# Background steps of an attention loop sorted by the engine they need, and a layernorm's small operations on GpSimd

## The chip, the cores and the metric

The kernel runs on one core of one Trainium2 chip. The metric is the device time of one launch in microseconds (us), the median of several runs. The core's engines are TensorE (PE; its weight loads are listed as PEld), VectorE (DVE), ScalarE (ACT), GpSimd (POOL) and SyncE (SP), which issues the DMAs. Each engine works through its own queue in order.

## The reference, cut to what matters

```python
x = x + 0.5 * ffn(layernorm(x))          # x: 4 batches of 1024 tokens, 128 wide
x = x + attn(layernorm(x))
x = x + 0.5 * ffn(layernorm(x))
# attn: its own layernorm h of its input (with scale and bias); c_q, c_kv = h @ w_down.T (64 latents each);
#       16 heads of 64 from the latents, rope on q and k, softmax(q k / 8) v, w_out, plus its input
# ffn:  8 experts; router weights from sigmoid(x @ Wr / temperature), zone test, a top-2 fallback;
#       sum over experts of weight * (silu(x Wg) * (x Wu)) Wd
# layernorm: (x - mean) / sqrt(var + 1e-5)
```

All is float32. The attention scores of 64 (batch, head) pairs over 1024 x 1024 tokens are the bulk of the work.

## The kernel before, in words

The program runs in three stages: the first feed-forward layer (until about 250 us), the attention loop (until about 1610 us) and the second feed-forward layer. The order on every engine is written out by hand: nothing is rescheduled.

**The attention loop** (in `run`) has groups g = 0 to 128 of four score slots each. A slot is one pair of heads, 512 queries and 128 keys. A unit is 8 slots, so two groups; a batch is 128 slots, so 32 groups. In each group, for n = 0 to 15, TensorE makes one matmul for each of two heads of the scores (`score`, L700: high and low parts of Q and K, then the maximum's row); at the fourth of a slot ScalarE takes the exponential (L704) and, with both heads done, GpSimd adds it to a sum (`accumulate`, L716). Between them, at n = 0, 7, 13 and behind n = 15, `passA` makes scores for the row maxima of a later unit in the two banks `psA` (L675) and VectorE reduces them (L676); the next such matmul must wait for that reduction, as there is one pair of banks. Then come the rope's matmuls (L595, even groups) or the output projection (`outp`, L756, odd groups), the fourth maximum, a background step, in even groups the denominator (`den`, L735, which reads GpSimd's sum), then VectorE's part of the rope (L583, four products) or of the output (L764, eight adds), and last the values of the four slots before (`values`, L723, into bank `psC`). The banks of the scores go round over `psS[0..3]` and `psX`; rope and output use `psX` and `psS[3]`; `den` uses `psS[0]`, and the steps' own matmuls get `self.rest = [self.psS[1]]` through `aux`.

GpSimd also has two rope sums (L600, L602) and a remainder (L611) in every second group. SP issues, in its order, the Q/K loads of later head pairs (16 in two groups), the latents for the rope, its stores, the maximum's way through DRAM (L679 to maxr) and the denominator's (L741, L743, read as dT by L760).

**Background steps** are generators that yield between steps. `attn_pre(b)` for batches 1 to 3 makes the two layernorms and the latents of a batch: statistics (`stats`: `bn_stats` L209, `bn_aggr` L212, the addition of EPS L213, all VectorE), `power` (L216, GpSimd, variance to the power -1/2), `norm` (L222 on VectorE forms -mean times that power, then ScalarE L227 applies it), transposes (L540), latents (L546, VectorE L552 and L553 split them into a high and a low part), a transpose of the key latents (L561) and the stores to `c_scr`. Each half of a batch has its own stages, 9 steps apart. `ffn_pre` does the same for the second feed-forward layer (transposes L256, router logits L269), then `route` (L293 to L348: ScalarE, GpSimd and a dozen small VectorE operations) and `weight_rows` (L357). It starts for batches 0, 1 and 2 in groups 42, 74 and 106.

`step(boundary)` picks a step in turn from the two streams (1: `ffn_pre`, 2: `attn_pre`). A generator yields True ahead of a step that needs TensorE; such a step runs only at `step(True)`, at the group's end. `step(False)` stands at n = 7 and n = 13. So there are three steps a group at most. For batches 2 and 3, `attn_pre` waits at stage 24 until the batch before last is done, and yields True until then.

In the first stage `bg1` and in the last `bg2` call the same generators by fixed rates.

Of the kernel before, what the change touches and what calls it, by code (L numbers as in the profile page):

```python
# [30 lines left out]
PBUFS = 8  # L31
NROPE = 9
# [5 lines left out]
class Kernel:  # L38
# [165 lines left out]


    def stats(self, st, src, mv, rstd, half):
# [3 lines left out]
        if half:  # L210
            for i in range(4):
                nc.vector.bn_aggr(mv[:, i, :], st[:, i, :])  # L212
            nc.vector.tensor_scalar(rstd[:, :, 1], mv[:, :, 1], EPS, None, ALU.add)  # L213

    def power(self, rstd):
        self.nc.gpsimd.tensor_tensor(rstd[:, :, 0], rstd[:, :, 1], self.neghalf[:, :4], ALU.pow)  # L216

    def norm(self, out, src, mv, rstd, half, vector=False):

        nc = self.nc  # L220
        if not (half or vector):
            nc.vector.scalar_tensor_tensor(rstd[:, :, 1], mv[:, :, 0], -1.0, rstd[:, :, 0], ALU.mult, ALU.mult)  # L222
# [7 lines left out]
    def ffn_pre(self, P, blks, xs, w_out, done=None, rows=None):  # L230
# [8 lines left out]
        def stage(k, h, blk):  # L239
# [5 lines left out]
            if k in (0, 1):  # L245
                self.stats(st["st", h], src, mv[:, hs], rstd[:, hs], k)
            elif k == 3:
                self.power(rstd[:, hs])
# [23 lines left out]
        for k in range(14 + 5 * (n - 1)):  # L272
            yield any(k - 5 * h in (8, 12) for h in range(n))
# [7 lines left out]
    def route(self, P, T, z, w_out):  # L281
# [9 lines left out]
        more = (None,) if self.slot >= 0 else ()  # L291
        yield
# [3 lines left out]
        yield  # L296
# [11 lines left out]
        yield  # L308
        v.reciprocal(dx, dx)
        yield  # L310
# [5 lines left out]
        yield  # L316
# [6 lines left out]
        yield  # L323
        g = new("g", [E, E], "f0")
        v.tensor_tensor(g, fb.unsqueeze(2).to_broadcast(sh4), below, ALU.is_gt)
        yield
        v.tensor_reduce(le, g, AX.X, ALU.add)
        yield
# [6 lines left out]
        yield  # L335
# [6 lines left out]
        yield  # L342
        v.tensor_tensor(w, w, fb, ALU.add)
        v.tensor_reduce(s, w, AX.X, ALU.add)
        yield
# [4 lines left out]
    def weight_rows(self, P, b):  # L350
# [4 lines left out]
        yield True  # L355
# [4 lines left out]
        yield  # L360
# [141 lines left out]
    def attn_pre(self, b):  # L502
# [9 lines left out]
        def stage(k, h):  # L512
# [6 lines left out]
            if k in (0, 1):  # L519
                assert 2 * b + h in self.done  # L520
                self.stats(st["st", h], src, mv[:, q], rstd[:, q], k)
            elif k == 2:
                self.power(rstd[:, q])
# [4 lines left out]
            elif k in (7, 8):  # L528
                self.stats(st["st", h], [y[:, i, :] for i in range(4)], mv2[:, q], rstd2[:, q], k - 7)
            elif k == 9:  # L530
                self.power(rstd2[:, q])
# [32 lines left out]
        for k in range(25 + 9):  # L564
            yield any(k - 9 * h in (14, 17, 20, 24) for h in range(2))
            while k == 24 and b >= 2 and self.slot < 128 * (b - 1) + 4:
                yield True
# [159 lines left out]
    def den(self, U):  # L727
# [3 lines left out]
        pd = self.psS[0]  # L731
# [36 lines left out]
    def run(self):  # L768
# [93 lines left out]
        self.rest, self.rope_banks, self.bankO = [self.psS[1]], [self.psX, self.psS[3]], [self.psX, self.psS[3]]  # L862
# [4 lines left out]
        def step(boundary):  # L867

            for _ in range(2):
                k = 1 + turns["next"] % 2  # L870
                turns["next"] += 1
                while streams[k] and streams[k][0] not in needs:
# [3 lines left out]
                    else:  # L876
                        needs[streams[k][0]] = v
                if streams[k] and (boundary or not needs[streams[k][0]]):
                    gen = streams[k][0]
# [139 lines left out]
```

## Time and profile before

| | us |
|---|---|
| median of 3 runs | 1769.61 (1763.7, 1769.61, 1775.22) |
| the profiled execution's own time | 1774.69 |
| its span, first to last instruction | 1772.9 |
| PE busy in the span | 1677.2 (95%) |
| DVE busy | 1304.0 (74%) |
| ACT busy | 925.2 (52%) |
| POOL busy | 1460.5 (82%) |
| row maxima on DVE, L676, 512 of 1224 ns | 626.7 |
| sums on POOL, L716, 320 of 2375 ns and 64 of 2390 ns | 912.9 |
| values on PE, L723, 2048 of 604 ns | 472.7 |

The profile is of one execution. Busy time is the sum of an engine's instructions; matmuls overlap, so a busy PE is not a PE at its peak. The waits view names, for each line, what ended the idle time before it. The windows view gives busy time in chosen stretches, with the granted clock of TensorE. Line numbers are those of the kernel before, unless the text says otherwise.

### The profile page before, as it was taken

The page shows a single profiled execution, that of the slowest core. Times are in us where ns is not written, and L with a number is a line of the kernel's source. Part 1 is how long each engine was busy: PE and PEld are TensorE (multiplying, and loading weights), DVE is VectorE, ACT ScalarE, POOL GpSimd, SP SyncE. Part 2 cuts the span into 40 slices and gives each one's busy share as a digit, 9 for nine tenths or more (in the row PEclk, how much of TensorE's full clock was granted, in tenths as well). Part 3 has the DMA queues.
Part 4 walks back from the last instruction along what each step waited for, and adds up shares of the span by engine and source line. Part 5 has one row for each costly group of instructions (what it writes and reads, how often), then busy time and mean ns, then how long its engine had stood idle before and what let it go on. Part 6 is the DMA issues. An engine that isn't in the chain of part 4 may idle for free.

```text
span 1772.9 us, 31230 instructions
## 1 busy us (share of the span) xinstructions
PE 1677.2 (95%) x11428; PEld 1043.0 (59%) x11428; DVE 1304.0 (74%) x2223; ACT 925.2 (52%) x1916; POOL 1460.5 (82%) x803
## 2 busy tenths in 40 slices
PE   7988978999999999999999999999999999899998
PEld 5777755555455555455555555655655555456777
DVE  6776658777777778777887777787777766744887
ACT  4666554556455455455444555544555544445555
POOL 4448778989889989889989899898999977576666
PEclk9999989999999999999999999999999999999999
DMA  6025446554544554445445545544545542024443
GB/s 200 1 72 175 134 131 155 144 144 120 143 121 121 135 153 120 120 132 144 117 115 139 146 126 147 131 125 112 130 121 148 127 98 61 2 86 109 141 124 103
DMA packets 241417, 216.00 MB, mean 122 GB/s; under 512 B 156784, under 2 KB 169712, under 8 KB 240624
## 3 DMA queue, kind: packets, MB, share of 16 engines
q1 hardware_dynamic: 241264, 214.01, 44.9%
q8 instruction: 90, 1.47, 0.4%
q14 instruction: 63, 0.52, 0.1%
HBM read 129.93 MB, written 84.02 MB: 121 GB/s over the span
## 4 chain that ended last, share of the span: by engine, by line
PE 72%; DVE 12%; POOL 5%; ACT 3%; issue 3%; DMA 2%; SPq 2%; POOLq 0%; DVEq 0%; ACTq 0%
PE psc L723 21%; PE ps_s L700 17%; PE ps_a L675 9%; PE psx L700 5%; DVE m L676 4%; PE ps_s L402 3%; PE ps_s L735 3%; PE ps_s L481 3%; POOL acc L716 2%; PE psx L436 2%; PE psx L756 2%; SPq L47 2%; PE psx L595 2%; DVE X L764 1%; PE psc L373 1%
## 5 line engine op out<-in xcount | busy, mean ns | idle before, releaser
L676 DVE TENSOR_REDUCE m<-ps_a 128x2 f32<-128x1024 f32 x512 | 626.7, 1224 | 327.5 <-PE ps_a L675 326.6
L716 POOL TENSOR_TENSOR acc<-acc,p 128x1024 f32<-128x1024 f32 x320 | 760.0, 2375 | 53.7 <-ACT p L704 34.5
L704 ACT ACTIVATE p<-ps_s 128x512 f32<-128x512 f32 x896 | 494.2, 599 | 370.2 <-PE ps_s L700 359.5
L700 PE MATMUL ps_s<-QT,KT 64*128 64x512 f32 x2688 | 478.1, 398 | 3.1 <-DVE X L764 2.1
L723 PE MATMUL psc<-p,ckn 128*64 128x512 f32 x2048 | 472.7, 604 | 0.0
L700 PEld LDWEIGHTS ps_s<-QT,KT 64*128 64x128 f32 x2688 | 314.5, 187 | 50.7 <-DVE X L764 3.4
L723 PEld LDWEIGHTS psc<-p,ckn 128*64 128x64 f32 x2048 | 136.8, 138 | 266.4 <-issue 265.5
L675 PE MATMUL ps_a<-KT,QT 64*128 64x512 f32 x1024 | 247.8, 476 | 37.5 <-DVE m L676 37.4
L716 POOL TENSOR_TENSOR acc<-p 128x1024 f32<-128x1024 f32 x64 | 152.9, 2390 | 98.0 <-ACT p L704 98.0
L675 PEld LDWEIGHTS ps_a<-KT,QT 64*128 64x128 f32 x1024 | 98.7, 185 | 208.6 <-DVE m L676 95.8
L700 PE MATMUL ps_s<-maxr,one_row 64*128 64x512 f32 x896 | 206.2, 394 | 0.0
L611 POOL TENSOR_TENSOR eo<-eo,hi_r 128x1024 fp32r<-128x1024 f32 x64 | 153.2, 2394 | 1.4 <-ACT hi_r L607 1.3
L725 ACT COPY osb<-psc 128x512 f32<-128x512 f32 x64 | 37.6, 587 | 189.0 <-PE psc L723 189.0
L386 POOL TENSOR_TENSOR X<-X,dtmp 128x512 f32<-128x512 f32 x54 | 69.2, 1282 | 66.1 <-ACT dtmp L385 59.6
L700 PE MATMUL psx<-QT,KT 64*128 64x512 f32 x384 | 111.9, 398 | 0.0
L700 PEld LDWEIGHTS ps_s<-maxr,one_row 64*128 64x128 f32 x896 | 99.7, 186 | 11.5
L489 POOL TENSOR_TENSOR p<-eo,p 128x512 fp32r<-128x512 f32 x42 | 63.0, 1505 | 43.8 <-ACT p L488 35.8
L600 POOL TENSOR_TENSOR eo<-rt,rt 128x512 f32<-128x512 f32 x64 | 82.8, 1294 | 5.5 <-DVE rt L583 5.4
L602 POOL TENSOR_TENSOR eo<-rt,rt 128x512 f32<-128x512 f32 x64 | 82.4, 1288 | 0.0
L764 DVE SCALAR_TENSOR_TENSOR X<-ps_s,rT,X 128x128 f32<-128x128 f32 x252 | 70.9, 344 | 13.5 <-PE ps_s L756 7.5
L700 PEld LDWEIGHTS psx<-QT,KT 64*128 64x128 f32 x384 | 72.1, 188 | 12.1
L704 ACT ACTIVATE p<-psx 128x512 f32<-128x512 f32 x128 | 77.6, 606 | 1.2 <-ACT p L704 0.6
(195 smaller groups left out, 2502.5 us busy)
## 6 DMA issues: line engine op xcount, KB each, us to landing
C_l<-cs SPq DMA_DIRECT2D x64, 512.0 KB
QT<-qs SPq DMA_DIRECT2D x256, 128.0 KB
KT<-ks SPq DMA_DIRECT2D x256, 128.0 KB
qs<-hi_r SPq DMA_DIRECT2D x32, 512.0 KB
qs<-eo SPq DMA_DIRECT2D x32, 512.0 KB
ks<-hi_r SPq DMA_DIRECT2D x32, 512.0 KB
ks<-eo SPq DMA_DIRECT2D x32, 512.0 KB
wb<-wt SPq DMA_DIRECT2D x64, 256.0 KB
```

The source lines that it names most:

```text
L386: nc.gpsimd.tensor_tensor(X[:, t:t + 4, :], X[:, t:t + 4, :], tmp, ALU.add)
L489: (nc.gpsimd if m < N - 1 else nc.vector).tensor_tensor(sh[:, 1, :], hp, self.f(sh[:, 0, :]), ALU.subtract)
L600: nc.gpsimd.tensor_tensor(w["eo"][:, 0, :], w[0, 0], w[1, 1], ALU.subtract)
L602: nc.gpsimd.tensor_tensor(w["eo"][:, 1, :], w[0, 1], w[1, 0], ALU.add)
L611: nc.gpsimd.tensor_tensor(w["eo"].bitcast(F32R), w["eo"], self.f(w["hi"]), ALU.subtract)
L675: nc.tensor.matmul(self.psA[:, hh, :], self.QT[P % 3][r, 0, q0:q0 + 128], self.KT[P % 3][r, 0, kk * 512:kk * 512 + 512], start=True, stop= ...
L676: nc.vector.tensor_reduce(self.m_of[U][:, :, qb, kk], self.psA, AX.X, ALU.max)
L700: nc.tensor.matmul(ps, w, x, start=k == 0, stop=k == 3)
L704: nc.scalar.activation(self.p_of[s][:, hh, :], ps, AF.Exp, scale=0.125)
L716: nc.gpsimd.tensor_tensor(acc, self.p_of[s - 1] if c == 1 else acc, self.p_of[s], ALU.add)
L723: nc.tensor.matmul(self.psC[64 * hh:64 * hh + 64, :], self.ckn[b % 2][:, c, :], self.p_of[s][:, hh, :], start=c == 0, stop=c == 7)
L764: nc.vector.scalar_tensor_tensor(x, po[hh][:, i * 128:(i + 1) * 128], rT[:, 4 * hh + i:4 * hh + i + 1], x, ALU.mult, ALU.add)
```

## The change

`stats` no longer adds EPS, and `norm` no longer forms the product L222. `power` does both on GpSimd: it adds EPS, takes the power, multiplies by the mean and by -1, four instructions instead of one.

Every yield now names a kind: OTHER (ScalarE, GpSimd, DMA or nothing), VECTOR, or PE. `step(most)` takes a step whose kind is at most `most`; of two it prefers one of kind PE. It stands at n = 7 (OTHER), at the group's end (PE, so any) and behind the second of the four value slots (VECTOR). The call at n = 13 is gone. Stage 0, 1, 7 and 8 of `attn_pre` and 0 and 1 of `ffn_pre` (the statistics) and the VectorE steps of `route` are VECTOR; the steps with matmuls remain PE.

The second row maximum of a group moves from n = 7 to n = 6. The steps' matmuls and the denominator take banks from `aux` by turns, now `psS[0]` and `psS[1]`, counted anew in each group: the first taker gets `psS[0]`.

The rest of the diff renames yields in `route` and `weight_rows` (a plain yield, or one of `more`, becomes OTHER or VECTOR by the engine of the step that follows; the True of `weight_rows` becomes PE).

```diff
@@ -29,6 +29,7 @@
 NGRP = NSLOT // 4
 DIRECT = 1
 PBUFS = 8
+OTHER, VECTOR, PE = 0, 1, 2
 NROPE = 9
 ACTS = (4, 6, 7)
 WLAG, GS, GD = 4, 17, 22
@@ -202,24 +203,29 @@
             nc.vector.tensor_copy(self.G[:, 4 * n:4 * n + 4, :], ps.rearrange("p (j d) -> p j d", j=4))
             yield
 
-
-    def stats(self, st, src, mv, rstd, half):
+    def kind(self, at, vector, pe):
+
+        return PE if any(k in pe for k in at) else VECTOR if any(k in vector for k in at) else OTHER
+
+
+    def stats(self, st, src, mv, half):
         nc = self.nc
         for i in (0, 1) if not half else (2, 3):
             nc.vector.bn_stats(st[:, i, :], src[i])
         if half:
             for i in range(4):
                 nc.vector.bn_aggr(mv[:, i, :], st[:, i, :])
-            nc.vector.tensor_scalar(rstd[:, :, 1], mv[:, :, 1], EPS, None, ALU.add)
-
-    def power(self, rstd):
-        self.nc.gpsimd.tensor_tensor(rstd[:, :, 0], rstd[:, :, 1], self.neghalf[:, :4], ALU.pow)
+
+    def power(self, mv, rstd):
+        nc = self.nc
+        nc.gpsimd.tensor_scalar(rstd[:, :, 1], mv[:, :, 1], EPS, None, ALU.add)
+        nc.gpsimd.tensor_tensor(rstd[:, :, 0], rstd[:, :, 1], self.neghalf[:, :4], ALU.pow)
+        nc.gpsimd.tensor_tensor(rstd[:, :, 1], mv[:, :, 0], rstd[:, :, 0], ALU.mult)
+        nc.gpsimd.tensor_scalar(rstd[:, :, 1], rstd[:, :, 1], -1.0, None, ALU.mult)
 
     def norm(self, out, src, mv, rstd, half, vector=False):
 
         nc = self.nc
-        if not (half or vector):
-            nc.vector.scalar_tensor_tensor(rstd[:, :, 1], mv[:, :, 0], -1.0, rstd[:, :, 0], ALU.mult, ALU.mult)
         for i in (0, 1) if not half else (2, 3):
             if vector:
                 nc.vector.tensor_scalar(out[:, i, :], src[i], mv[:, i, 0:1], rstd[:, i, 0:1], ALU.subtract, ALU.mult)
@@ -243,9 +249,9 @@
             if k == 0:
                 st["st", h] = self.small.tile([128, 4, 6], F32, name="st")
             if k in (0, 1):
-                self.stats(st["st", h], src, mv[:, hs], rstd[:, hs], k)
+                self.stats(st["st", h], src, mv[:, hs], k)
             elif k == 3:
-                self.power(rstd[:, hs])
+                self.power(mv[:, hs], rstd[:, hs])
             elif k in (5, 6):
                 if k == 5:
                     st["y", h] = P.tile([128, 4, 128], F32, name="yf", tag="f0")
@@ -270,7 +276,7 @@
                 nc.vector.tensor_reduce(z[:, hs, :], pz[:, 0:64].rearrange("p (t k e) -> p t e k", t=4, k=2), AX.X, ALU.add)
 
         for k in range(14 + 5 * (n - 1)):
-            yield any(k - 5 * h in (8, 12) for h in range(n))
+            yield self.kind([k - 5 * h for h in range(n)], (0, 1), (8, 12))
             for h, blk in enumerate(blks):
                 stage(k - 5 * h, h, blk)
         yield from self.route(P, 4 * n, z, w_out)
...
@@ -562,9 +568,9 @@
                 nc.vector.tensor_copy(self.ckn[b % 2][:, 4 * h:4 * h + 4, :], pt[:, 0:256].rearrange("p (t l) -> p t l", t=4))
 
         for k in range(25 + 9):
-            yield any(k - 9 * h in (14, 17, 20, 24) for h in range(2))
+            yield self.kind([k - 9 * h for h in range(2)], (0, 1, 7, 8), (14, 17, 20, 24))
             while k == 24 and b >= 2 and self.slot < 128 * (b - 1) + 4:
-                yield True
+                yield PE
             for h in range(2):
                 stage(k - 9 * h, h)
 
@@ -728,7 +734,7 @@
 
         nc = self.nc
         osb = self.osb_of[U] = self.op2.tile([128, 512], F32, name="osb")
-        pd = self.psS[0]
+        pd = self.aux()
         parts = [self.p_of[8 * U + c] for c in range(8 - DIRECT, 8)] + [self.acc_of[U]]
         for k, part in enumerate(parts):
             for n in range(4):
@@ -859,30 +865,34 @@
         for _ in streams[2].pop() if streams[2] else ():
             pass
         assert not (streams[0] or streams[2])
-        self.rest, self.rope_banks, self.bankO = [self.psS[1]], [self.psX, self.psS[3]], [self.psX, self.psS[3]]
+        self.rest, self.rope_banks, self.bankO = self.psS[:2], [self.psX, self.psS[3]], [self.psX, self.psS[3]]
         streams[2] += [self.attn_pre(b) for b in range(1, B)]
         turns = {"next": 0}
         needs = {}
 
-        def step(boundary):
-
-            for _ in range(2):
-                k = 1 + turns["next"] % 2
-                turns["next"] += 1
+        def step(most):
+
+
+            turns["next"] += 1
+            found = []
+            for i in range(2):
+                k = 1 + (turns["next"] + i) % 2
                 while streams[k] and streams[k][0] not in needs:
                     v = next(streams[k][0], self)
                     if v is self:
                         streams[k].pop(0)
                     else:
-                        needs[streams[k][0]] = v
-                if streams[k] and (boundary or not needs[streams[k][0]]):
-                    gen = streams[k][0]
-                    v = next(gen, self)
-                    if v is self:
-                        streams[k].pop(0)
-                    else:
-                        needs[gen] = v
-                    return
+                        needs[streams[k][0]] = v or OTHER
+                if streams[k] and needs[streams[k][0]] <= most:
+                    found.append(k)
+            if found:
+                k = max(found, key=lambda k: needs[streams[k][0]] == PE)
+                gen = streams[k][0]
+                v = next(gen, self)
+                if v is self:
+                    streams[k].pop(0)
+                else:
+                    needs[gen] = v or OTHER
 
 
         ROPE = {"mid": {2: "dhi"}, "side": {0: "mm"}, "end": {-1: "fetch", 0: "o0 o1 e0 e1 e o", 2: "dlo"}, "cast": {1: "hi0 hi1 lo"}}
@@ -901,8 +911,8 @@
             maxima = lambda i: self.passA(s0 + AHEAD + i) if s0 + AHEAD + i < NSLOT else None
 
             for n in range(16):
-                if n in (0, 7, 13):
-                    maxima((n + 1) // 7)
+                if n in (0, 6, 13):
+                    maxima((n + 1) // 6)
                 if g < NGRP:
                     s, k = divmod(n, 4)
                     for hh in range(2):
@@ -910,8 +920,7 @@
                 if n == 7:
                     rope(g, "mid")
                     self.run_later(g, "mid")
-                if n in (7, 13):
-                    step(False)
+                    step(OTHER)
             rope(g, "side")
             self.run_later(g, "side")
             maxima(3)
@@ -919,7 +928,8 @@
             b, i = divmod(s0, 128)
             if i == 40 and 1 <= b < B:
                 streams[1].append(pre2(b - 1))
-            step(True)
+            self.nrest = 0
+            step(PE)
             if g and g % 2 == 0:
                 self.den(g // 2 - 1)
             rope(g, "end")
@@ -937,6 +947,8 @@
             for s in range(s0 - 4, s0):
                 if s >= 0:
                     self.values(s)
+                if s == s0 - 3:
+                    step(VECTOR)
         for i in range(2):
             for k in range(2):
                 for hl in range(2):
```

More of the change, by code (lines that the diff above doesn't have):

```diff
@@ L290, in route @@
         inh, dist = new("inh", [E]), new("dist", [E])
-        more = (None,) if self.slot >= 0 else ()
-        yield
+        more = (VECTOR,) if self.slot >= 0 else ()
+        yield OTHER
         act(inh, z[:, :T], AF.Tanh, scale=self.rtemp)
@@ L295, in route @@
         act(dist, inh, AF.Abs, bias=self.consts[:, 1:2])
-        yield
+        yield OTHER
         ex = P.tile([128, 2, TPB, E], F32, name="ex")[:, :, :T]
@@ L307, in route @@
         pool.tensor_tensor(ge, ge, le, ALU.mult)
-        yield
+        yield VECTOR
         v.reciprocal(dx, dx)
-        yield
+        yield OTHER
         pool.tensor_tensor(ex, ex, dx, ALU.mult)
@@ L315, in route @@
         pool.tensor_tensor(below, fb.unsqueeze(3).to_broadcast(sh4), self.tri.unsqueeze(1).to_broadcast(sh4), ALU.mult)
-        yield
+        yield VECTOR
         v.tensor_tensor(w, w, ge, ALU.mult)
@@ L322, in route @@
         v.tensor_scalar(some, s, 1e-8, None, ALU.is_ge)
-        yield
+        yield VECTOR
         g = new("g", [E, E], "f0")
         v.tensor_tensor(g, fb.unsqueeze(2).to_broadcast(sh4), below, ALU.is_gt)
-        yield
+        yield VECTOR
         v.tensor_reduce(le, g, AX.X, ALU.add)
-        yield
+        yield VECTOR
         v.scalar_tensor_tensor(fb, le, 2.0, fb, ALU.is_lt, ALU.mult)
@@ L334, in route @@
         v.tensor_scalar(r, r, 1e-8, None, ALU.max)
-        yield
+        yield VECTOR
         v.reciprocal(r, r)
@@ L341, in route @@
         v.tensor_tensor(fb, fb, bc(r), ALU.mult)
-        yield
+        yield VECTOR
         v.tensor_tensor(w, w, fb, ALU.add)
         v.tensor_reduce(s, w, AX.X, ALU.add)
-        yield
+        yield VECTOR
         v.tensor_scalar(s, s, 1e-8, 2.0, ALU.max, ALU.mult)
@@ L359, in weight_rows @@
         nc.scalar.copy(wt, ps[0:64, 0:128])
-        yield
+        yield OTHER
         nc.sync.dma_start(out=self.wt_scr[b].rearrange("e (t p) -> (e t) p", p=128), in_=wt)
@@ L520, in stage @@
                 assert 2 * b + h in self.done
-                self.stats(st["st", h], src, mv[:, q], rstd[:, q], k)
+                self.stats(st["st", h], src, mv[:, q], k)
             elif k == 2:
-                self.power(rstd[:, q])
+                self.power(mv[:, q], rstd[:, q])
             elif k in (4, 5):
@@ L528, in stage @@
             elif k in (7, 8):
-                self.stats(st["st", h], [y[:, i, :] for i in range(4)], mv2[:, q], rstd2[:, q], k - 7)
+                self.stats(st["st", h], [y[:, i, :] for i in range(4)], mv2[:, q], k - 7)
             elif k == 9:
-                self.power(rstd2[:, q])
+                self.power(mv2[:, q], rstd2[:, q])
                 nc.gpsimd.tensor_tensor(X[:, t0:t0 + 4, :], X[:, t0:t0 + 4, :], y, ALU.add)
@@ L564, in attn_pre @@
         for k in range(25 + 9):
-            yield any(k - 9 * h in (14, 17, 20, 24) for h in range(2))
+            yield self.kind([k - 9 * h for h in range(2)], (0, 1, 7, 8), (14, 17, 20, 24))
             while k == 24 and b >= 2 and self.slot < 128 * (b - 1) + 4:
-                yield True
+                yield PE
             for h in range(2):
```

## The prediction, made before the changed kernel ran

> **What bounds the kernel now.** I read the page's sums and its chain shares first, then the windows table over stretches of 16 groups, then the timeline and the chain inside single groups, and last the waits and the rows of the lines that the change touches. A group is one pass of the attention loop (four score slots); each is marked by its sixteen value matmuls (L723).
>
> ```profile
> PE 1677.2 (95%) x11428; PEld 1043.0 (59%) x11428; DVE 1304.0 (74%) x2223; ACT 925.2 (52%) x1916; POOL 1460.5 (82%) x803
> PE 72%; DVE 12%; POOL 5%; ACT 3%; issue 3%; DMA 2%; SPq 2%; POOLq 0%; DVEq 0%; ACTq 0%
> ```
>
> TensorE carries the chain (72%), VectorE is second (12%). The windows show where (us, then busy PE, PEld, DVE, ACT, POOL, clock, DMA share, GB/s):
>
> ```profile
> 255.40:349.50 94.10, 87.97 (x620) 50.36 (x618) 71.53 (x116) 51.75 (x103) 81.62 (x42) 0.98 0.54 142
> 349.50:523.80 174.30, 168.56 (x1221) 96.49 (x1220) 132.19 (x225) 91.46 (x180) 157.71 (x79) 0.99 0.49 132
> 523.80:687.40 163.60, 163.60 (x1214) 95.08 (x1212) 125.22 (x207) 85.69 (x166) 153.43 (x74) 1.00 0.50 134
> 687.40:871.40 184.00, 172.67 (x1238) 98.45 (x1236) 138.09 (x229) 96.05 (x193) 163.97 (x85) 0.98 0.51 134
> 871.40:1041.00 169.60, 165.84 (x1215) 94.60 (x1213) 131.49 (x196) 83.47 (x160) 151.25 (x73) 0.99 0.49 127
> 1041.00:1216.70 175.70, 167.51 (x1227) 96.68 (x1225) 139.42 (x222) 88.64 (x176) 157.93 (x80) 0.99 0.50 131
> 1216.70:1377.10 160.40, 160.40 (x1201) 93.22 (x1200) 116.94 (x176) 83.79 (x161) 152.08 (x73) 1.00 0.51 129
> 1377.10:1550.80 173.70, 163.49 (x1191) 93.49 (x1189) 123.63 (x198) 83.45 (x166) 131.25 (x63) 0.99 0.31 70
> ```
>
> The first row is 8 groups, the others 16 each. The stretch at 1216.7 has no background step: 160.4 us, TensorE never idle, 10.03 us a group. Against that the others lose 13.9 + 13.9 + 3.2 + 23.6 + 9.2 + 15.3 + 13.3 = 92.4 us. The steps' own matmuls take part of this (L546 1.07 us in the chain, 12 of them, 12.8; the 27 smaller ones 0.25 to 0.65 each by their starts, about 12): 24.9. So **67.5 us are stalls** that the steps cause. One of them, in the chain:
>
> ```profile
> 1200.43 2.32 DVE wts L348
> 1202.75 1.10 DVE m L676
> 1203.85 0.04 issue
> 1203.89 0.50 PE ps_a L675 x2
> ```
>
> A routing step stands between two row maxima on VectorE; TensorE waits until the second maximum frees ps_a. Where VectorE is free, in an undisturbed group:
>
> ```profile
> 1249.34 0.68 DVE L583 TENSOR_TENSOR rt<-psx,sin 128x512 f32<-128x512 f32 x1
> 1251.42 1.23 DVE L676 TENSOR_REDUCE m<-ps_a 128x2 f32<-128x1024 f32 x1 [1.40 <-PE ps_a L675]
> 1253.27 1.23 DVE L676 TENSOR_REDUCE m<-ps_a 128x2 f32<-128x1024 f32 x1 [0.63 <-PE ps_a L675]
> ...
> 1260.92 1.23 DVE L676 TENSOR_REDUCE m<-ps_a 128x2 f32<-128x1024 f32 x1 [0.42 <-PE ps_a L675]
> ```
>
> During the values VectorE has 1.40 us free in even groups (behind the rope's products) and 0.42 in odd ones (behind the output's adds); between maxima inside the scores 0.4 to 0.6.
>
> **The change, part by part.**
>
> *Small operations.* 32 additions of EPS (L213) and 31 products (L222) leave VectorE; GpSimd runs four operations for one at each power. In the attention (from 255 us):
>
> ```profile
> L213 DVE TENSOR_SCALAR rstd<-mv x11: 170/718/1879, 267.0 to 738.1; 128x4 f32<-128x4 f32 x11
> L222 DVE SCALAR_TENSOR_TENSOR rstd<-mv,rstd x12: 156/1055/2223, 254.8 to 775.0; 128x4 f32<-128x4 f32 x12
> L216 POOL TENSOR_TENSOR rstd<-rstd,neghalf x16: 1007/1020/1033, 71.5 to 748.6; 128x4 f32<-128x4 f32 x16
> ACT ya L227 <- DVE rstd L222: 27.8, 12, 4.2
> ```
>
> The shortest take 0.17 us, the longest 1.9 to 2.2, near one accumulation on GpSimd (2.375 us): they are held there. The Trainium skill's page "GPSIMD Engine Reference" (Key points) says that GpSimd shares its SBUF interfaces with VectorE, with contention against two-input or two-port VectorE instructions; the trace agrees (0.17 against 2.2 us). Gone with them is ScalarE's wait for L222 (27.8 and 9.4 us), behind which exponentials stood. Each power now costs GpSimd 1.02 + 3 x about 0.35 (L305 0.383, L307 0.322, both larger): +1.05, 18 times in the attention, 19 us. GpSimd is the fullest engine there: 152 of 160.4 us. It is not late in an undisturbed pair (it waits 132.6 us in all for ScalarE's p), and the sums are read by the denominator some 5 us after the last addition. Bounds 0 to 19 us; I take **+3**, near 0 because of that margin. ScalarE's norms now wait for GpSimd: two to three steps later, 6 to 10 us, hidden unless GpSimd is behind.
>
> *Placement.* By the order of the two programs, each group still has three chances, but the two inside the scores (n = 7, 13) become one that takes only ScalarE/GpSimd/DMA steps, and VectorE steps go to the group's end or among the values, both in the one gap of 1.40 or 0.42 us (4.1 in even groups from 110 on, where the rope's four 0.68 are over), plus the time of TensorE work in the same step. What does not fit delays the first maximum and stalls TensorE. Costs from the rows: statistics 2 x 0.28, with the aggregation 1.16; cast and remainder (L552, L553) 1.38; routing steps by their medians in the attention (L320 to L322 3.38, L325 1.90, L327 0.67, L336 and L337 1.36, L339 1.68, L341 1.37, L343 and L344 1.60, L346 to L348 2.67).
> - attn_pre: group 3 (0.56 + 1.16 - 0.42 = 1.3), 19 and 41 likewise 1.3; 23, 45, 47 (1.38 + 1.16 - 0.42 - 1.07 = 1.05); 15, 18, 37, 40, 43 some 0.3 each; others 0.2: 8.8.
> - Routing of batch 0: at the group's end the waiting attn_pre takes most turns (groups 51 to 65), so one VectorE step a group: 60 2.0, 61 1.5, 65 0.9, 67 1.3, 69 1.3, 70 1.3: 8.3.
> - Batch 1, two a group: 74 and 76 0.3 each, 77 and 83 0.5 each, 84 2.2, 85 2.15, 87 2.6, 88 1.6, 89 2.25: 12.4.
> - Batch 2: the same, its routing in odd groups only (even ones have 4.1): 8.7.
>
> Stalls after: 38.2 us, against 67.5: **-29.3**. The waits that steps had behind exponentials (bank psS[1]; 4.3 us at L540, 3.3 at L546) and late output sums (rT <- DMA dT 24.1 us, six times) lie inside the 67.5; I count none after. If they stay, 10 us come back.
>
> *Maximum at n = 6 for 7.* Undisturbed, TensorE waits about 0.1 us at n = 13 now and would wait it at n = 6: 0. After a late first maximum it loses up to 0.13 more, in 25 groups: **+2** (0 to 4).
>
> *Banks.* A step's matmul goes to psS[0], whose exponential is two slots older, the denominator then to psS[1]; both are emptied during the values (3.6 us): 0, up to +1 per step if the copy is late, 27 steps.
>
> *DMAs.* The c_scr and x2 stores, the weight row's too, move with their steps on SP, past the Q/K loads and dsb; each issue is 0.4 to 0.8 us, the longest 3.4 (at 469.8). Latents of batch 1 are stored in groups 8 to 13, read from 13 on: 0, at worst two outputs late, 8 us (groups 21 and 41 lost 3.9 and 4.1 so).
>
> *Before and behind the attention.* Until 255 us GpSimd is busy 162, 12 powers add 12.6 us there; VectorE loses some 17; ScalarE waited 8.7 for L222. Start: the first power stands on the path, +1. I take 0 in all, bounds -8 to +8. The tail has two powers: 0.
>
> Sum: -29.3 + 3 + 2 = -24.3. The profiled run took 1774.7 us (span 1772.9); that is 5.1 over the median of 1769.6. So 1750.4 in such a run, **1745** at the median.
>
> **The rivals.**
> - *Held VectorE steps eat the gain.* If every small routing operation costs a whole GpSimd addition (2.38) instead of its median, the three routings stall 34 us more; half of that, 17, gives 1762. For: L348 2264 to 2320 each time. Against: L339 215, L322 157 once. The Trainium skill's page "GPSIMD Engine Reference" (Key points), taken strictly, would give the full 34 and 1779; the medians do not bear it out.
> - *ScalarE behind GpSimd (slower).* A norm stands in front of exponentials; power waits behind two accumulations (4.75) and a rope remainder (2.4), more with the X add. The place: groups 4, 20, 42 and the norms right after a power. From 1.35 us of stall at each of 18 norms the gain is gone; with 2.5 each (45 us) it ends at 1790. For: GpSimd 95% busy, one stretch (group 3) lost 7.5 us to a late norm before. Against: the distance of 6 us or more, ScalarE half idle.
> - *The steps' stalls vanish more fully.* Routing operations at their whole-kernel means (L322 0.72, L339 0.62, L348 1.27) the 38.2 fall by 15, and the first stage gives its 8: 1722.
>
> **How the numbers follow.** The forecast 0.45 (1735 to 1755), full vanishing 0.18, held steps 0.23, ScalarE behind GpSimd 0.14. A measurement of this kernel tells about 1% from no change. Faster by over 1% (under 1752): the full case, and most of the forecast (0.41): 0.59. Same: 0.04 of the forecast, the held steps 0.23: 0.27. Slower: 0.14. The range 1720 to 1776 leaves out most of the slow rival and little below.
>
> **What would show it.** In the windows the stretches of batch 1 and 2 routing fall only by 0 to 3 us, those at 255 to 523 by about 14 and at 687 to 1041 by about 12. Waits of L675 for m (92.0 on PEld, 34.9 on PE) fall by a third or more; stalls sit before the second maximum, not the third or fourth. ScalarE's norms wait for GpSimd, under 15 us in all. Wrong it would be if the denominator waits for acc, if norms wait over 2 us each, or if the undisturbed stretch is not 160.4 again.

## The result and the profile after

The changed kernel takes **1748.09 us** (median of four runs, 1746.33 to 1748.73) against 1770.17 us of the kernel before (four runs, those shown and one more): a ratio of 0.988 [0.984, 0.991], 22 us less. The profiled execution took 1747.59 us, with a span of 1745.8 us: 27.1 under the span before, where the prediction's sum was -24.3. In the rest of the text "after" is this kernel; its lines have numbers about six higher than those of before (the maxima are L681 and L682, the scores L706, the sums L722, the values L729, the output's adds L770).

The page of after, busy time by engine and the chain's shares by engine:

```profile
PE 1664.3 (95%) x11428; PEld 1055.8 (60%) x11428; DVE 1266.5 (73%) x2160; ACT 925.5 (53%) x1916; POOL 1484.7 (85%) x899
PE 70%; DVE 16%; POOL 4%; issue 3%; ACT 3%; DMA 2%; SPq 2%; DVEq 0%; POOLq 0%; ACTq 0%
```

GpSimd gained 24.2 us and 96 instructions, VectorE lost 37.5 us and 63 instructions, as the code says. VectorE's share of the chain did not fall, it rose from 12 to 16%. One number fits nothing in the prediction: weight loads (PEld) are as many as before and 12.8 us longer. Both come back below.

The windows of after, cut at the same groups as those of before (8 groups, then 16 each), and the 14 groups of the seventh window that have no background step:

```profile
252.90:337.80 84.90, 83.82 (x610) 48.81 (x608) 61.52 (x106) 47.11 (x94) 82.39 (x54) 1.00 0.56 145
337.80:507.50 169.70, 168.31 (x1231) 99.32 (x1230) 127.85 (x221) 94.34 (x185) 161.02 (x91) 1.00 0.52 141
507.50:672.70 165.20, 164.35 (x1215) 97.92 (x1214) 121.96 (x198) 86.62 (x167) 155.75 (x77) 1.00 0.51 135
672.70:845.40 172.70, 169.13 (x1240) 99.91 (x1238) 126.62 (x218) 93.87 (x188) 165.86 (x96) 1.00 0.53 139
845.40:1016.90 171.50, 165.40 (x1215) 98.24 (x1213) 136.26 (x201) 85.64 (x168) 154.52 (x78) 1.00 0.49 128
1016.90:1190.90 174.00, 165.94 (x1228) 98.61 (x1226) 133.54 (x214) 88.48 (x177) 159.22 (x86) 1.00 0.52 131
1190.90:1356.20 165.30, 163.60 (x1205) 97.72 (x1203) 119.72 (x179) 84.07 (x163) 152.20 (x73) 0.99 0.51 128
...
1214.80:1356.20 141.40, 141.40 (x1053) 84.82 (x1052) 102.38 (x154) 73.49 (x142) 132.94 (x64) 1.00 0.53 134
1356.20:1523.50 167.30, 161.57 (x1192) 95.26 (x1190) 120.91 (x190) 83.32 (x166) 133.05 (x69) 1.00 0.32 73
```

Stretch by stretch, after minus before: -9.2, -4.6, +1.6, -11.3, +1.9, -1.7, +4.9, -6.4, together -24.8 us. Ahead of the first group it is -2.5, behind the last window +0.2. The stretches in which most layernorms of `attn_pre` lie (the first, second and fourth) give -25.1 of it; those with the routing (the fifth, sixth and eighth) give -6.2, which the third and the seventh take back. The third, fifth and seventh stretch became longer. The seventh was the undisturbed one: its last routing step slipped in from the stretch before (the chain below), and even its 14 undisturbed groups take 10.10 us each where before they took 10.03.

The waits of after, from 250 to 1600 us (engine, line and what it waited for: us in total, times, longest):

```profile
PEld ps_a L681 <- DVE m L682: 94.4, 178, 2.2
PE ps_a L681 <- DVE m L682: 25.6, 34, 1.7
ACT ya L233 <- POOL rstd L224: 5.7, 3, 3.7
```

TensorE's waits for the row maxima are 120.0 us; they were 126.9 (from 255 to 1606 us of before). ScalarE's norms waited 27.8 us for VectorE at `ya` and 9.4 at `yf`; now they wait 5.7 for GpSimd at `ya`, and no wait of `yf` for it is listed.

The last routing step of batch 1 in after (group 89), in the chain:

```profile
1192.74 2.28 DVE wts L354
...
1197.35 1.14 DVE m L682
1198.49 0.04 issue
1198.53 0.50 PE ps_a L681 x2
...
1200.67 0.43 PE psx L706
...
1203.36 0.23 PE ps_s L601
```

The routing operation (L348 before, L354 now, 2.28 us) stands among the values, as the change wants it. The output's adds follow it, then the first maximum of the next group, which ends at 1198.5, and only then can TensorE go on. So the stall was not taken away there but moved, from ahead of the third maximum to ahead of the second. The score matmuls behind it then take 0.43 us a pair for some 4 us, where the rope's matmuls of the same width behind them (L601) take 0.23: the windows view of after gives a mean granted clock of 0.63 from 1198.5 to 1203.1, with 1.00 on both sides.

### The profile page after: what moved, and what is told of

Read it like the earlier page. It is cut to its first block, busy times and chain, and to the rows that moved or that the text cites. A ratio compares the mean times of both kernels' runs of the same rounds, so it can differ in the third digit from the quotient of the medians.

```text
span 1745.8 us, 31261 instructions
## 1 busy us (share of the span) xinstructions
PE 1664.3 (95%) x11428; PEld 1055.8 (60%) x11428; DVE 1266.5 (73%) x2160; ACT 925.5 (53%) x1916; POOL 1484.7 (85%) x899
## 4 chain that ended last, share of the span: by engine, by line
PE 70%; DVE 16%; POOL 4%; issue 3%; ACT 3%; DMA 2%; SPq 2%; DVEq 0%; POOLq 0%; ACTq 0%
PE psc L729 18%; PE ps_s L706 17%; PE ps_a L681 9%; PE psx L706 5%; DVE m L682 5%; DVE X L770 3%; PE ps_s L741 3%; PE ps_s L408 3%; PE ps_s L487 3%; PE ps_s L762 2%; PE psx L601 2%; PE psx L442 2%; DVE rt L589 1%; SPq L48 1%; PE psc L379 1%
## 5 line engine op out<-in xcount | busy, mean ns | idle before, releaser
L682 DVE TENSOR_REDUCE m<-ps_a 128x2 f32<-128x1024 f32 x512 | 627.3, 1225 | 343.3 <-PE ps_a L681 343.2
L722 POOL TENSOR_TENSOR acc<-acc,p 128x1024 f32<-128x1024 f32 x320 | 761.5, 2380 | 36.6 <-ACT p L710 17.0
L706 PE MATMUL ps_s<-QT,KT 64*128 64x512 f32 x2688 | 503.9, 396 | 1.3 <-ACT p L710 0.6
L729 PE MATMUL psc<-p,ckn 128*64 128x512 f32 x2048 | 467.7, 598 | 0.0
L706 PEld LDWEIGHTS ps_s<-QT,KT 64*128 64x128 f32 x2688 | 327.4, 185 | 36.9 <-issue 2.4
L729 PEld LDWEIGHTS psc<-p,ckn 128*64 128x64 f32 x2048 | 135.6, 136 | 262.5 <-issue 261.5
L681 PE MATMUL ps_a<-KT,QT 64*128 64x512 f32 x1024 | 255.0, 469 | 30.1 <-DVE m L682 29.3
L681 PEld LDWEIGHTS ps_a<-KT,QT 64*128 64x128 f32 x1024 | 98.2, 184 | 201.9 <-DVE m L682 99.8
L722 POOL TENSOR_TENSOR acc<-p 128x1024 f32<-128x1024 f32 x64 | 152.7, 2386 | 75.3 <-ACT p L710 75.2
L706 PE MATMUL ps_s<-maxr,one_row 64*128 64x512 f32 x896 | 214.0, 392 | 0.0
L706 PEld LDWEIGHTS ps_s<-maxr,one_row 64*128 64x128 f32 x896 | 107.8, 185 | 10.6
L706 PE MATMUL psx<-QT,KT 64*128 64x512 f32 x384 | 110.1, 392 | 0.0
L770 DVE SCALAR_TENSOR_TENSOR X<-ps_s,rT,X 128x128 f32<-128x128 f32 x252 | 71.0, 344 | 12.8 <-PE ps_s L762 7.4
L706 PEld LDWEIGHTS psx<-QT,KT 64*128 64x128 f32 x384 | 70.8, 185 | 12.2
```

The source lines that it names most:

```text
L681: nc.tensor.matmul(self.psA[:, hh, :], self.QT[P % 3][r, 0, q0:q0 + 128], self.KT[P % 3][r, 0, kk * 512:kk * 512 + 512], start=True, stop= ...
L682: nc.vector.tensor_reduce(self.m_of[U][:, :, qb, kk], self.psA, AX.X, ALU.max)
L706: nc.tensor.matmul(ps, w, x, start=k == 0, stop=k == 3)
L722: nc.gpsimd.tensor_tensor(acc, self.p_of[s - 1] if c == 1 else acc, self.p_of[s], ALU.add)
L729: nc.tensor.matmul(self.psC[64 * hh:64 * hh + 64, :], self.ckn[b % 2][:, c, :], self.p_of[s][:, hh, :], start=c == 0, stop=c == 7)
L770: nc.vector.scalar_tensor_tensor(x, po[hh][:, i * 128:(i + 1) * 128], rT[:, 4 * hh + i:4 * hh + i + 1], x, ALU.mult, ALU.add)
```

## The experiments

All ratios are to the kernel before, measured beside the run, with a 95% interval.

| run | us | ratio |
|---|---|---|
| after | 1748.09 | 0.988 [0.984, 0.991] |
| after, second maximum at n = 7 again (e1) | 1736.98 | 0.981 [0.975, 0.986] |
| after, small operations on VectorE again (e2) | 1784.95 | 1.009 [1.006, 1.012] |
| after, old places, n = 6 (e3) | 1744.39 | 0.985 [0.980, 0.990] |
| after, old banks (e4) | 1747.90 | 0.988 [0.983, 0.993] |
| before, with the small operations on GpSimd (e5) | 1747.72 | 0.988 [0.986, 0.990] |
| before, second maximum at n = 6 (e6) | 1772.23 | 1.000 [0.998, 1.002] |
| before, with the new places alone (e7) | 1774.33 | 1.005 [1.003, 1.007] |
| after, only EPS on VectorE (e8) | 1760.94 | 0.997 [0.995, 0.999] |
| after, only the product on VectorE (e9) | 1772.48 | 1.003 [1.001, 1.005] |
| e3 with n = 7 (e11) | 1743.85 | 0.984 [0.982, 0.986] |
| e9, product as four 128x1 operations (e12) | 1751.07 | 0.991 [0.988, 0.993] |
| e1, small routing operations on GpSimd too (e10) | 1720.98 | 0.971 [0.969, 0.973] |

**The four parts, each undone.** The theory was the prediction's: the gain comes from the places. The rival: it comes from the small operations that left VectorE.

e1, the second maximum back at n = 7:

```diff
-                if n in (0, 6, 13):
-                    maxima((n + 1) // 6)
+                if n in (0, 7, 13):
+                    maxima((n + 1) // 7)
```

> The changed kernel with the second row maximum back at n = 7. In the changed kernel's profile an undisturbed pair of groups takes 20.2 us against 20.05 before, and the stretch without steps shows the two heads' matmuls for the third maximum 0.09 us apart. Theory: the move to n = 6 costs 0.09 us in each of 126 groups, so this kernel is 9 to 11 us faster than the changed one, about 1738, and its undisturbed pair is 20.05 again. Rival (the prediction's term, +2 us for late maxima alone, nothing in undisturbed groups): 1746, and the longer pair comes from the other banks or another part of the change and stays at 20.2.

Measured 1736.98 us: n = 6 costs 11 us, where the forecast had 2. The 14 undisturbed groups of e1, in its windows view, answer to the row 1214.80 of after:

```profile
1205.10:1345.40 140.30, 140.30 (x1051) 81.39 (x1049) 102.17 (x154) 73.22 (x142) 133.26 (x64) 1.00 0.52 133
```

That is 1.1 us less over 14 groups with nothing in them, so the price is there in every group: 0.08 us each, and all eight stretches of e1 are 0.8 to 2.3 us shorter. Weight loads are 3.4 us shorter in this window, and their waits for the row maxima too. The waits view over these 14 groups, of after and then of e1:

```profile
PEld ps_a L681 <- DVE m L682: 7.7, 21, 0.4
```

```profile
PEld ps_a L681 <- DVE m L682: 4.9, 21, 0.4
```

Twenty-one waits in both. Seven, of the fourth maximum in every second group, are 0.37 us in both. The other fourteen moved and grew: in before and in e1 the third maximum's weight load (n = 13) waits 0.16 us, in after the second's (n = 6) waits 0.37. The weight loads of one group of before, and one of after, in the timeline:

```profile
1254.55 0.19 PEld L675 LDWEIGHTS ps_a<-KT,QT 64*128 64x128 f32 x2 [0.16 <-DVE m L676]
```

```profile
1240.43 0.19 PEld L681 LDWEIGHTS ps_a<-KT,QT 64*128 64x128 f32 x2 [0.37 <-DVE m L682]
```

Of these 2.8 us over 14 groups, 1.1 reach the groups' time; PE's own column shows no idle time in either. The third maximum's two matmuls, one for each head, which run side by side, also start 0.09 us apart in after (the mean of 13 undisturbed groups), and under 0.01 apart in e1 and in before; what makes that skew is not settled.

e2, both small operations on VectorE again:

```diff
+            nc.vector.tensor_scalar(rstd[:, :, 1], mv[:, :, 1], EPS, None, ALU.add)
...
-        nc.gpsimd.tensor_scalar(rstd[:, :, 1], mv[:, :, 1], EPS, None, ALU.add)
...
-        nc.gpsimd.tensor_tensor(rstd[:, :, 1], mv[:, :, 0], rstd[:, :, 0], ALU.mult)
-        nc.gpsimd.tensor_scalar(rstd[:, :, 1], rstd[:, :, 1], -1.0, None, ALU.mult)
...
+            nc.vector.scalar_tensor_tensor(rstd[:, :, 1], mv[:, :, 0], -1.0, rstd[:, :, 0], ALU.mult, ALU.mult)
```

> The changed kernel with the addition of EPS and the product of mean and power back on VectorE; placement, banks and n = 6 stay. Theory (prediction): in the attention 17 additions at 0.7 to 1.0 us and 18 products at 0.9 to 1.1 us return to VectorE; the additions lie in the gap at the values where about half of them find no room (some 8 us), the products stand in front of ScalarE's norms, some of them inside the scores (6 to 10 us): 12 to 18 us slower than the changed kernel, 1760 to 1766, with ScalarE's norms waiting for VectorE some 30 us again. Rival (placement alone made the gain, and GpSimd's added 19 us cost as much as VectorE's relief brings): within 4 us of 1748.

Measured 1784.95 us: 37 us over after and slower than before. The direction was the rival's, the size more than either theory had.

e3, the steps back in their old places:

```diff
-                    step(OTHER)
+                if n in (7, 13):
+                    step(VECTOR)
...
-                if s == s0 - 3:
-                    step(VECTOR)
```

> The changed kernel with the old places of the steps: VectorE steps allowed at n = 7 and n = 13 again, none among the values; small operations on GpSimd, banks and n = 6 stay. Theory (prediction): placement made the larger part of the gain, so this loses 10 to 16 us against the changed kernel, 1758 to 1764, with stalls of row-maximum matmuls inside the scores again. Rival (the small operations made the gain, placement only moved the stalls from the scores to the values): within 4 us of 1748.

Measured 1744.39 us, 3.7 under after, with intervals that overlap: without the new places nothing is lost. The theory fell here.

e4, the old banks (`self.rest = [self.psS[1]]`, `pd = self.psS[0]`):

> The changed kernel with the old banks: the steps' matmuls in psS[1] alone, the denominator in psS[0]. Theory (prediction): the waits of steps' matmuls behind exponentials came from late norms, which are gone, so the banks are worth 0 to 4 us: 1748 to 1752, with PE waits at the steps' matmuls for exponentials under 3 us. Rival: the banks took away the 8 us of such waits seen before: 1756, and these waits return.

Measured 1747.90 us: the banks are worth nothing in these places, as forecast.

**Each part alone.** e5 is the kernel before with the new `stats`, `power` and `norm` and nothing else:

> The kernel before with one part of the change alone: the addition of EPS and the product on GpSimd. Old places, old banks, maximum at n = 7. Theory (formed after the first four runs: the small operations made the whole gain, the places none, the move to n = 6 cost 9): 1733 to 1738, some 35 us under the kernel before, and as fast as the changed kernel with the maximum at n = 7 (1737) or a little faster. Rival (the small operations pay only where the steps are placed anew): 1745 to 1755.

Measured 1747.72 us, 18 under the 1765.7 of the kernel before beside it: the small operations alone give as much as the whole change. It is 10 us above what was expected of it, so the operations are not all of the story either. One difference from the kernels with the new places is ScalarE's wait for GpSimd's power. The waits view of e5, from 250 to 1600 us:

```profile
ACT ya L228 <- POOL rstd L219: 16.8, 6, 5.2
```

With `yf` it is 19.3 us; in e3 and e11, which have the old places too, `ya` waits 17.9 and 18.1, but 5.7 in after and 4.4 in e1. So once the operations are on GpSimd, the new places bring the norms less waiting. How much of that reaches TensorE is not shown.

e7 is the kernel before with the new places alone (small operations on VectorE, old banks, n = 7):

> The kernel before with the new places of the steps alone: small operations on VectorE, old banks, maximum at n = 7. Theory (the places alone gain nothing): the kernel with everything but the small operations took 1785, of which 9 by n = 6, so 1776 here, 6 us over the kernel before. Rival (the prediction: the places are the main part of the gain of 29): 1750 to 1760.

Measured 1774.33 us, 0.3 to 0.7% over before. The prediction gave the places -29.3 us; alone they cost 8. The windows of its profiled execution, the longest of its ten (1783.28 us), show where: the stretch of groups 40 to 55, 184.0 us before and 172.7 after, takes 190.3. The routing stretches do become shorter, groups 72 to 87 172.1 for 175.7 and groups 104 to 119 167.5 for 173.7, with 3.9 more in the stretch between them.

e6 is the kernel before with e1's edit the other way round, the second maximum at n = 6:

> The kernel before with the second row maximum at n = 6 alone. Theory A (the cost of the move lies in the undisturbed group, 0.07 us each, and adds up with any placement): 6 to 9 us slower than before, 1775 to 1779 beside a before of 1769. Theory B (with steps still standing at n = 7, the move gives the step one more pair of matmuls' time behind the maximum, which pays the cost back): within 3 us of before, or some us faster; the undisturbed pair is 20.2 all the same, and the stretches with steps are shorter than before.

Measured 1772.23 us, a ratio of 1.000: no cost. Its undisturbed stretch has the cost all the same (161.5 us against 160.4), but the stretches in which routing steps stand at n = 7, right behind the second maximum, are shorter: groups 72 to 87 173.8 against 175.7, groups 104 to 119 171.0 against 173.7. So with the old places n = 6 pays itself back, and with the new ones, where no VectorE step stands at n = 7, only the cost is left. e11 is the other test of that, e3 with n = 7:

> The kernel with the small operations on GpSimd and the new banks, steps at n = 7 and 13 as before (with the new order of choice, steps of kind PE first at the end), and now the maximum at n = 7. With n = 6 it took 1744, the small operations alone with old banks and old choice 1748. Theory A (n = 6 costs 9 everywhere): 1735. Theory B (n = 6 pays itself back where VectorE steps stand at n = 7): 1743 to 1749, so that the new places are worth 6 to 12 us once the small operations are gone (1737 with new places and n = 7).

Measured 1743.85 us against e3's 1744.39. By stretches it is the same exchange: undisturbed 160.4 against 161.6, routing 175.8 against 171.9 and 173.5 against 169.9.

**Why two operations of 0.15 us cost 37.** Theory: a small VectorE operation that starts while GpSimd is in an instruction ends only when that one ends. In the trace of before, the timeline at 288 us (start, us, engine, line):

```profile
287.96 2.35 POOL L716 TENSOR_TENSOR acc<-acc,p 128x1024 f32<-128x1024 f32 x1
```

```profile
288.10 2.22 DVE L222 SCALAR_TENSOR_TENSOR rstd<-mv,rstd 128x4 f32<-128x4 f32 x1
```

GpSimd's sum ends at 290.31, the product (its shortest is 0.156) at 290.32. The routing operation of the prediction's chain, L348 from 1200.43 to 1202.75, is the same: the sum that ran beside it ended at 1202.62.

```profile
1200.24 2.38 POOL L716 TENSOR_TENSOR acc<-p 128x1024 f32<-128x1024 f32 x1 [3.52 <-ACT p L704]
```

Over the attention of before, 32 of the 35 operations of L213 and L222 end 0.02 to 0.08 us behind the end of the GpSimd instruction in which they began; two of the other three began together with a sum, within 0.01 us, and took 0.16 and 0.17. Together they take 33.2 us, where 35 times 0.17 would be 6. Reductions, reciprocals, `bn_stats`, `bn_aggr` and operations with an operand in PSUM keep one duration throughout (the reciprocal L336 0.18 to 0.19 beside the same sums). The Trainium skill's page "GPSIMD Engine Reference" (8. Key points) names contention with VectorE instructions of two SBUF inputs or a two-port mode. The trace agrees for the operations with two SBUF inputs (L222, L348); in which mode the additions (L213, one input) run, no row shows. The price in these rows is the rest of the running GpSimd instruction, up to 2.2 us. e8 and e9 put one operation back each, by the lines of e2's diff:

> The changed kernel with only the addition of EPS back on VectorE (the product stays on GpSimd). Both back cost 37 us. Theory (what hurts is VectorE held by GpSimd in front of ScalarE: the norm waits for the product, and the exponentials behind the norm wait too): the additions stand behind the aggregation and in front of the row maxima only, so they cost their own time where it does not fit, 17 of about 0.9 us: 5 to 12 us, 1753 to 1760. Rival (only VectorE's held time counts, and it is about the same for both): 15 to 20 us, 1763 to 1768.

> The changed kernel with only the product of mean and power back on VectorE (EPS stays on GpSimd). Theory (the norm behind a held product stops ScalarE and with it the exponentials): 22 to 32 us, 1770 to 1780, with ScalarE's norms waiting for VectorE some 30 us and more stalls of the row-maximum matmuls. Rival (held time alone): 15 to 20 us, 1763 to 1768.

Measured 1760.94 and 1772.48 us: 12.9 and 24.4 over after, 37.3 together, which is e2's 37 (by the ratios, as the kernel before was faster beside these two, 17 and 27, together 44, against 38). The addition costs 1 us more than its theory's range and less than its rival's, the product as much as its theory had. The product costs more than the addition. Some of that is a chain that grows: it is late for ScalarE's norm (the waits `ya <- rstd` are 29.1 us in e9), and SP can be late behind it. In e9 the step of group 41, from SP's queue, VectorE's timeline and the chain:

```profile
683.74 0.42 SPq L749 DMA_DIRECT2D dT<-d  x1
```

```profile
689.45 0.20 DVE L766 RECIPROCAL rT<-dT 128x8 f32<-128x8 f32 x1 [2.49 <-DMA dT<-d]
```

```profile
692.59 1.12 DVE m L682
693.71 0.04 issue
693.75 0.80 PE ps_a L681 x2
```

The load of dT is issued behind the eight Q/K loads before it (L48, 679.6 to 683.7) and is 5.68 us on the way, VectorE waits 2.49 us for it, the first maximum ends at 693.7, TensorE stands 2.08 us and then has a granted clock of 0.50 from 693.7 to 699.0. The group takes 16.2 us; in after it takes 11.7. That SP's lateness there goes back to a held product is argued, not shown by a row. The Trainium skill's page "TensorE: Matmul & The Clock Gate" (What's actually happening) says that the clock halves after an idle window of about 3.4 us. The trace agrees with a halved clock behind a stall (0.50 here, 0.63 on the mean of 4.6 us in group 89 of after), but the rows show shorter pauses ahead of it: 0.46 and 2.08 us here, 0.25 and 1.44 there, with some matmuls between.

e12 tests the hold by itself: the product stays on VectorE, in a form that is not held.

```diff
-            nc.vector.scalar_tensor_tensor(rstd[:, :, 1], mv[:, :, 0], -1.0, rstd[:, :, 0], ALU.mult, ALU.mult)
+            for i in range(4):
+                nc.vector.tensor_scalar(rstd[:, i, 1:2], mv[:, i, 0:1], rstd[:, i, 0:1], -1.0, ALU.mult, ALU.mult)
```

> As the changed kernel with only the product on VectorE (1772), but the one product of two 128x4 tiles is now four operations on 128x1, each with one tile and a per-partition scalar, in the same place. In the profile before, VectorE's short operations with two SBUF tiles, or with one tile of 128x4 or 128x8 and a constant, end 0.02 to 0.14 us behind the GpSimd instruction that runs beside them, whereas statistics, reductions, reciprocals and operations with one input in PSUM keep one duration. Theory (the hold hits two-tile operations and those that read one tile two elements at a time; a 128x1 operation is neither): four times 0.1 to 0.2 us, none over 0.3, so ScalarE's norms hardly wait and the time is 1750 to 1758. Rival (every short operation that reads and writes SBUF is held, or the extra stage on VectorE is what costs): the four take up to 2.4 us together and the time is 1768 to 1778.

Measured 1751.07 us: 21 under e9, with four instructions for one. The rows of the product in the attention, of e9 and then of e12 (min/median/max ns):

```profile
L228 DVE SCALAR_TENSOR_TENSOR rstd<-mv,rstd x12: 153/1709/2222, 259.0 to 758.7; 128x4 f32<-128x4 f32 x12
```

```profile
L229 DVE TENSOR_SCALAR rstd<-mv,rstd x44: 201/204/206, 285.7 to 740.9; 128x1 f32<-128x1 f32 x44
```

Four times 0.204 is longer than the shortest 0.153, and it never becomes longer. One part of the expectation was missed: ScalarE's norms still wait 20.5 us for the product (`ya` 16.0, `yf` 4.5, where e9 has 29.1 and 8.4). Still, the form alone brings back 21 of the 24 us: most of the price is the hold, not that VectorE has the work.

**What follows from it.** If the hold is the price, the small routing operations have it too (L354, 2.28 us above). e10 is e1 with these on GpSimd in the attention and the tail; VectorE keeps the reductions, the reciprocals and the comparison of 512 elements. Steps that now need GpSimd alone are of kind OTHER and may stand at n = 7, so for them the place changes with the engine. The core of the edit, where each part is a step of its own:

```diff
+            pool.tensor_scalar(le, le, 2.0, None, ALU.is_lt)
+            pool.tensor_tensor(fb, fb, le, ALU.mult)
...
+            pool.tensor_tensor(w, w, bc(some), ALU.mult)
+            pool.tensor_tensor(fb, fb, bc(r), ALU.mult)
+            pool.tensor_tensor(w, w, fb, ALU.add)
...
+            pool.tensor_tensor(w_out, w, bc(s), ALU.mult)
```

> The changed kernel with the maximum at n = 7 (1737) and, in the attention and after it, the small routing operations on GpSimd too: comparisons, the maxima with 1e-8, the products with flags, sums and weights; VectorE keeps the reductions, the reciprocals and the comparison of 512 elements. Same number of steps. Theory (a small VectorE operation beside a full GpSimd costs up to 2.4 us of held time, on GpSimd itself 0.2 to 0.4): of the routing's stalls, some 26 us in the changed kernel, two thirds go, GpSimd takes about 4 us more a batch: 1718 to 1726. Rival (GpSimd is full, what VectorE saves comes back as waits for GpSimd): 1733 to 1742, with VectorE's reductions or the denominator waiting for GpSimd.

Measured 1720.98 us, as the theory had it: 16 under e1, 27 under after, 2.7 to 3.1% under before. It is the best of all. Its page has VectorE at 6% of the chain where e1 has 11% and after 16%, and its waits for the maxima fall to 61.1 us on PEld, from e1's 75.2:

```profile
PE 76%; POOL 10%; DVE 6%; issue 4%; ACT 3%; DMA 1%; SPq 1%; POOLq 0%; DVEq 0%; ACTq 0%
```

```profile
PEld ps_a L716 <- DVE m L717: 61.1, 201, 1.6
```

```profile
L355 POOL TENSOR_TENSOR wts<-ex,ws x4: 313/330/784, 925.8 to 1658.6; 128x64 f32<-128x64 f32 x4
```

The operation that held VectorE for 2.28 us takes GpSimd 0.33. How much of the 16 us comes from the engine and how much from the place of these steps was not separated.

## Why the prediction was right in its time and wrong in its reason

**The sum.** -24.3 forecast, -27.1 measured between the profiled spans, 1745 against 1748 at the median. That the time fits is luck, as errors cancel: the operations and the places together gave about -34 (e1, 0.981), the maximum at n = 6 took 11 of it back, and the reason given for the gain was not the one that the runs show.

**Placement, -29.3: the step that failed.** The prediction subtracted stalls after (38.2) from stalls before (67.5) and called the difference the worth of the places. But its 67.5 held the stalls of L213 and L222 (33.2 us of VectorE time), and its 38.2, worked out from the other steps' durations, did not. So the difference held, under the name of the places, what comes from the operations. The runs in place of it: the places alone +8 us (e7), the operations alone -18 (e5). The parts are not additive: from e7 to e1 the operations (and banks) bring about 42 us, from before to e5 18 to 21. The new places pay only once the held operations of the layernorm are off VectorE: e1 is 7 us under e11, which has the old places and n = 7 too (0.981 and 0.984, with intervals that overlap). The prediction's total of the stalls in the gaps, on the other hand, held up: worked out for after in the same way, stretch excess over undisturbed groups less the steps' matmuls, it is some 34 us against 38.2. Of what it counted away beside that, the steps' waits behind exponentials did go (7.6 us on PE at L540 and L546 before, none on PE after). The late output sums stayed, 23.6 us for 24.1, but they were never inside the 67.5: some 20 us of both lie in the last two outputs, behind the last window.

**Small operations, +3: the term with the wrong sign.** It counted only what GpSimd gets. That part was even too dear. The rows of after's four operations (lines view of each line, min/median/max ns):

```profile
L222 POOL TENSOR_TENSOR rstd<-rstd,neghalf x16: 1038/1039/1042, 71.3 to 729.3; 128x4 f32<-128x4 f32 x16
...
L221 POOL TENSOR_SCALAR rstd<-mv x16: 227/228/228, 71.0 to 729.0; 128x4 f32<-128x4 f32 x16
...
L223 POOL TENSOR_TENSOR rstd<-mv,rstd x16: 202/204/208, 72.4 to 730.4; 128x4 f32<-128x4 f32 x16
...
L224 POOL TENSOR_SCALAR rstd<-rstd x16: 239/239/239, 72.7 to 730.7; 128x4 f32<-128x4 f32 x16
```

0.23 + 0.20 + 0.24 is +0.67 for a power, not +1.05. For 18 powers it is 12 us, on an engine with a margin (the second fullest in the undisturbed stretch, behind TensorE, and not the fullest as the prediction has it), and the denominator waits for the sum twice, 2.9 us in all. The prediction had read the hold in the rows (0.17 against 2.2 us) and used it as a reason, but put no number on its going away.

**Maximum at n = 6, +2 (0 to 4): mis-sized.** It measured 11, and the 0 in undisturbed groups was the fault: the prediction took a wait of 0.1 us to move from n = 13 to n = 6 unchanged. It did move, but from 0.16 us to 0.37 in the weight loads (7.7 us of such waits against 4.9 over 14 groups), and 0.08 us of it is left in every group.

**Banks 0:** right (e4, -0.2 us). **DMAs 0:** no stretch shows a late store. **First stage and tail:** -2.5 us, inside -8 to +8, and -2.0 us where 0 was taken.

**The rivals.** ScalarE behind GpSimd did not come: 5.7 us of waits in three places, under the 15 named. With the old places it is 17.9 to 19.3 us (e3, e11, e5), and even there nothing was slower than before. Held VectorE steps are real (L354), but the medians in the sum already held them. The full vanishing, 1722 us, did not come with this change; e10 reached 1721 with the small routing operations on GpSimd as well.

**The signs.** Stretches 255 to 523: -13.8 us, forecast 14. From 687 to 1041: -9.4, forecast 12. Batch 1's routing -1.7, as forecast (0 to 3), but the stall of its last step, some 3.7 us, now lies in the stretch behind; batch 2's -6.4, twice the forecast. Waits of the maxima were to fall by a third and fell by 5% (126.9 to 120.0): n = 6 and the held routing steps in the gap kept them; e1 has 75.2 + 19.6, a quarter less. The undisturbed stretch was named as a test and failed it (10.10 us a group for 10.03): that was the sign of the n = 6 price, visible before any experiment. Two more of its signs of being wrong show on a small scale: the denominator waits for acc (the 2.9 us above), and one norm waits 3.7 us, over the 2 named.

**Open.** Why placement alone costs 8 us is only argued: the held operations then stand in the one gap, beside the output's adds, and group 41 may become late as it does in e9. e11 (0.984) is 0.5% under e5 (0.988), with the new banks and the choice of PE steps first; the two were not separated. Neither the longer wait at n = 6 nor the skew behind it is explained.

## What to carry to other kernels

Ahead of a change that moves work, split the stalls of the profile by the instruction that makes each of them, and subtract only those that the edit touches; a stretch's total credits whichever part comes to mind first. A small VectorE operation whose duration goes from 0.15 to 2.2 us beside a full GpSimd is being held: give it to GpSimd itself (0.2 to 0.4 us here, but 1.04 for a power) or write it in a form that keeps its duration, and sort the steps only after that. A cost in undisturbed groups, however small, is multiplied by their number: 0.08 us in each of some 130 groups was about 10 us here.

## What the runs showed of the hardware that was not expected

- The hold depends on the operation's form: 128x4 with two SBUF operands took 0.15 to 2.22 us, the same product as four 128x1 operations with a scalar from each partition 0.201 to 0.206 us each, in the same places.
- TensorE's granted clock fell to 0.50 and 0.63 behind recorded pauses of 2.08 and 1.44 us (means over 5.3 and 4.6 us, in e9 and in after), and matmuls there took 0.42 to 0.43 us a pair for 0.23.
- Moving a maximum by one position among the scores cost 0.08 us a group without any idle time on PE, with longer weight loads (84.82 against 81.39 us over 14 groups) and longer waits of theirs (7.7 against 4.9).
